# Residual add of the FFN by GpSimd, pieces of the Mamba chunks at other iterations, first chunk's load ahead of the weights, and strip rows one word longer

## The chip, the cores and the metric

The kernel runs on one core of a Trainium2 chip. A core has five engines with instruction streams of their own: TensorE (PE in the profile; its weight loads are PEld), VectorE (DVE), ScalarE (ACT), GpSimd (POOL) and SyncE (SP), which here only issues DMA transfers. They share an on-chip memory of 128 partitions (SBUF); TensorE writes to a second one (PSUM). The metric is the time of one execution on the device in microseconds (us); lower is better. Everything is computed in fp32.

## The reference, cut to what matters

The input x is 4 images of 64 channels and 128x128 pixels. Four layers follow each other:

```
layer 0: tokens of all images as ONE sequence of 65,536
         y = mamba(tokens, 16 states); p = proj(out_proj(y)); x = silu(layernorm(p)) + x
layer 1: q from the largest Sobel gradients; a windowed block transform by FFT, a block MLP
         with soft shrinkage, the transform back; + x
layer 2: r = relu(bn(conv3x3(relu(bn(conv3x3(x)))))); gate from means over cropped images;
         relu(r * gate + x)
layer 3: t = conv3x3(relu(conv3x3(x))) as tokens, 4 sequences of 16,384
         t = t + mamba(layernorm(t), 64 states)
         t = t + ffn(layernorm(t))       # 1x1 to 256, depthwise 3x3, GELU, 1x1 to 64
         x + t

mamba(u): xh, z = split(u @ in_w.T)                   # 128 channels each
          xc = silu(causal conv of 4 taps over xh)
          dt, B, C = split(xc @ x_proj.T)
          delta = softplus(dt @ dt_w.T + dt_b)
          h_t = h_{t-1} * exp(delta_t * A) + (delta_t * xc_t) B_t ;  y_t = h_t C_t
          (y + xc * D) * silu(z)
```

The recurrence in h runs over every channel and every state: 128 x 16 scans in layer 0, 128 x 64 in layer 3.

## The kernel before, in words

**Stages.** The layers run one after the other. In the profiled execution layer 0 lies at 0 to 3206 us, the gradients, window and transform of layer 1 at 3206 to 4280, the convolutions of layers 2 and 3 at 4283 to 5076, layer 3's Mamba at 5076 to 16,082, and its FFN at 16,082 to 17,159.

**The Mamba class.** Both Mamba layers use the class `_Mamba`. The tokens are cut into chunks of 1024, 64 chunks in each layer. An *iteration* is one scan instruction of VectorE (L640) over 1024 tokens on 128 partitions; these hold 4 states of 32 channels, and 4 iterations (j) make a *group* of 4 states of all 128 channels. A chunk has 16 iterations in layer 0 and 64 in layer 3. In each iteration ScalarE computes the decay `da` (an exponential, L595) up to six iterations ahead, TensorE brings the input term into a PSUM tile `bx`, VectorE scans it into a slot of `ring`, GpSimd multiplies the slot by the replicated C row (`cb`, L646), and TensorE later sums over the states into `y` (L470).

The input term has two kinds, written as a letter per group ("DADA" in layer 0, "DAAA" four times in layer 3). In a D group TensorE spreads B over the partitions (L533) and VectorE multiplies it by `du` (L539). In an A group the products with B are formed on transposed data: eight blocks of 128 tokens, each either one GpSimd instruction (L444, 512 elements) or four single ScalarE products (L440, 128 elements each), and then transposed by TensorE (L527). The number of blocks that GpSimd makes is `mine`: (2,) in layer 0, and (4, 2, 2) for the three A groups that follow a D group in layer 3.

Three PSUM tiles of 1024 columns (bx0 to bx2) are used in turn by the input terms and by the *pieces*: the matmuls that make the next chunk ready (convolution, z, delta, C, B, transposed du) or finish the last one (projection, LayerNorm). A piece is a generator: at a `yield` it hands over to the loop. `slots` gives, for each piece, the iteration after which it is issued, counted from the first iteration of its chunk: negative ones lie in the chunk before, those over 16 or 64 in the chunk after.

**What sets the order.** `run` writes the order out by hand, iteration by iteration: exponentials, products paced by a credit, the PSUM tiles to fill, the scan, GpSimd's product, y sums, pieces due, and replicated loads; `_Pin` fixes this order on each engine. All DMA transfers but those named below are issued by SP in program order.

**Front and start.** `front` computes xc (L321), sz (L330), pos (softplus, L339) and on GpSimd u = pos x xc (L347), and stores pos and u for the replicated loads. Its working tiles come from `tmp`. The constructor loads the weights by SP (L206 to L263, the 16 A_log transfers at L263 last), before anything of the first chunk. In layer 0 two chunks are then prepared ahead of the loop, in layer 3 one. Layer 3's `ahead` centres and normalises the tokens (on tile `nx`), and copies them by DMA into the convolution's input S; `behind` projects, adds the residual, normalises (tile `no`) and stores.

**Convolutions.** `layer2_convs3` works on strips of 16 rows. `strip` gives a tile of rows of 130 words (`RW` = 128 + 2). `_Conv.turned` forms four sums and differences V of rows, two on VectorE and two on GpSimd (L1233, L1235), which TensorE multiplies (L1247).

**FFN.** `layer3_ffn` has 32 strips of 16 rows. In each, hidden channels 128 to 255 are convolved by VectorE (`taps`, L1688 and eight L1686), the others by TensorE; `second` multiplies by fc2 and adds bias and residual (L1701) one strip later, and SP stores the result (L1704). `load` reads the normalised tokens two strips ahead (L1645). The residual tile `res` is loaded by SP from s3, and then x3 is added to it by four accumulating transfers issued by GpSimd (L1726). GpSimd then clears the borders of the next strip's hidden tile h (L1657, L1658, L1660), for which the next taps wait.

Of the kernel before, what the change touches and what calls it, by code (L numbers as in the profile page):

```python
# [10 lines left out]
F32 = mybir.dt.float32  # L11
AF = mybir.ActivationFunctionType
ALU = mybir.AluOpType
# [4 lines left out]
P = 128  # L18
B, C, HH, WW = 4, 64, 128, 128
HW = HH * WW  # L20
TC = 1024
# [149 lines left out]
class _Mamba:  # L171
# [18 lines left out]

    def __init__(self, ctx, tc, K, nst, w, kinds, bufs, slots={}):
        nc = self.nc = tc.nc
# [8 lines left out]

        self.slots = slots

        wx, xpd, dtw = (self.tmp(k)[:n, :DI] for k, n in (("wx", P), ("xpd", 4), ("dtw", 4)))
        for h in range(2):
# [15 lines left out]
        nc.sync.dma_start(self.wbc, w["xp_bcT"])  # L221
        self.small = nst <= DD
        self.wboth = cp.tile([P, NH, 64 if self.small else P], F32, name="wboth")
# [5 lines left out]
        self.spread = {}  # L229
        for g in (g for g, kind in enumerate(kinds) if kind == "D"):  # L230
# [74 lines left out]
    def tmp(self, name):  # L305
        return self.wp.tile([P, TC], F32, name=name, tag="tmp", bufs=self.bufs["tmp"])

# [170 lines left out]
    def run(self, chunks, ahead, behind, lead):  # L478
# [214 lines left out]
def layer0(ctx, tc, K, w, x, x1):  # L693
    nc = tc.nc
    slots = {"conv": -24, "z": -22, "v": -20, "C": -16, "B": -14, "duT": -12, "project": 32, "rstd": 34}
    m = _Mamba(ctx, tc, K, 16, w, "DADA", {"xc": 2, "sz": 3, "tmp": 4, "bc": 2, "soon": (), "da": 7, "made": 0, "mine": (2,)}, slots)
    cp, wp = m.cp, m.wp
    eps = cp.tile([P, 1], F32, name="eps")
    nc.vector.memset(eps, 1e-5)


    pw = cp.tile([64, 64], F32, name="pw")
    nc.sync.dma_start(pw, w["proj_w"])
    ow = cp.tile([64, DI], F32, name="ow")
    nc.sync.dma_start(ow, w["out_w"])
    pb = cp.tile([64, 1], F32, name="pb")
    nc.sync.dma_start(pb, w["proj_b"])
    pm = m.pm()
    nc.tensor.matmul(pm[:64, :64], pw, K.cent[:64, :64], start=True, stop=True)
    m1 = cp.tile([64, 64], F32, name="m1")  # L710
    nc.vector.tensor_copy(m1, pm[:64, :64])
    pm = m.pm()
    nc.tensor.matmul(pm[:, :64], ow, m1, start=True, stop=True)
    woT = cp.tile([P, 64], F32, name="woT")
    nc.vector.tensor_copy(woT, pm[:, :64])
    cent2 = cp.tile([64, P], F32, name="cent2")
    for h in range(2):
        nc.vector.tensor_copy(cent2[:, 64 * h : 64 * (h + 1)], K.cent[:64, :64])
    pm = m.pm()
    nc.tensor.matmul(pm[:, :1], cent2, pb, start=True, stop=True)  # L720
    ob = cp.tile([P, 1], F32, name="ob")
    nc.vector.tensor_copy(ob, pm[:, :1])
    lng = _dup(nc, cp, w["ln_g"], "lng")
    lnb = _dup(nc, cp, w["ln_b"], "lnb")

    finish = []
# [53 lines left out]

    chunks = [{"at": divmod(i * TC, HW), "reset": i == 0} for i in range(B * HW // TC)]
    m.run(chunks, ahead, behind, 24)
    flush()

# [491 lines left out]
def layer2_convs3(ctx, tc, K, w, w3, x2, x3, t3):  # L1276
# [202 lines left out]
def layer3_mamba(ctx, tc, K, w, t3, s3, n3):  # L1479

    nc = tc.nc
    slots = {"centre": -47, "norm": -45, "conv": -32, "conv2": -31, "z": -30, "v": -29, "C": -16, "B": -14, "duT": -12, "project": 80, "centre2": 82, "norm2": 84}
    m = _Mamba(ctx, tc, K, 64, w, "DAAADAAADAAADAAA", {"xc": 1, "sz": 2, "tmp": 4, "bc": 1, "soon": (), "da": 7, "made": 7, "mine": (4, 2, 2)}, slots)
    cp = m.cp
    eps = cp.tile([P, 1], F32, name="eps3")
    nc.vector.memset(eps, 1e-5)
    woT = cp.tile([P, 64], F32, name="woT")
# [10 lines left out]
    def load(c):  # L1498
        b, t0 = c["at"]
        X = c["X"] = m.t("X", 1, 512)  # L1500
        for h, src in enumerate(_halves(t3[b], t0)):
            nc.sync.dma_start(X[64 * h : 64 * (h + 1)], src)

    def ahead(c):
        if c is chunks[0]:
            load(c)
# [32 lines left out]
    def behind(c, yg):  # L1539
# [30 lines left out]

    chunks = [{"at": (b, t0), "reset": t0 == 0} for b in range(B) for t0 in range(0, HW, TC)]
    m.run(chunks, ahead, behind, 48)
# [3 lines left out]
def layer3_ffn(ctx, tc, K, w, n3, s3, x3, out):  # L1576
# [139 lines left out]
    for n, (b, r0) in enumerate(strips):  # L1716
# [6 lines left out]
        ximg = x3[b].rearrange("c (r w) -> c r w", w=WW)  # L1723
        for eng, img, add in ((nc.sync, simg, ALU.bypass), (nc.gpsimd, ximg, ALU.add)):
            for q in range(R // 4):
                eng.dma_start(res[half[q % 2], q // 2], img[:, r0 + 4 * q : r0 + 4 * q + 4, :], accum_op=add)  # L1726
        g0 = [wp.tile([P, 4, WW], F32, name=f"g0{q}", tag=f"g0{q}") for q in range(NR)]
# [129 lines left out]
```

## Time and profile before

| | |
|---|---|
| time, median of 3 runs | 17,136.39 us (17,125.25 to 17,164.81) |
| the profiled execution's own time | 17,161.19 us |
| its span | 17,159.4 us |
| busy: TensorE / VectorE / ScalarE / GpSimd | 80% / 89% / 80% / 81% |
| layer 0, a chunk | 48.65 us, VectorE idle 2.15 |
| layer 3 Mamba, a chunk | 170.66 us, VectorE idle 6.97 |
| FFN, a strip | 33.5 us |
| first scan of layer 0 / of layer 3 | 77.21 us / 5153.48 us |

The profile has one row for each group of instructions: line, engine, operation, output from inputs with their shapes, count, then busy time in all and mean ns of one, then the idle time before them and what ended most of it. A row of a timeline gives start and length in us, engine, line, operation, and in brackets how long the engine had waited and for what. A row of waits gives who waited for whom, the us in all, how often, and the longest. A row of windows gives the stretch, its length, and the busy time of each engine with the number of instructions.

### The profile page before, as it was taken

The page shows a single profiled execution, that of the slowest core. Times are in us where ns is not written, and L with a number is a line of the kernel's source. Part 1 is how long each engine was busy: PE and PEld are TensorE (multiplying, and loading weights), DVE is VectorE, ACT ScalarE, POOL GpSimd, SP SyncE. Part 2 cuts the span into 40 slices and gives each one's busy share as a digit, 9 for nine tenths or more (in the row PEclk, how much of TensorE's full clock was granted, in tenths as well). Part 3 has the DMA queues.
Part 4 walks back from the last instruction along what each step waited for, and adds up shares of the span by engine and source line. Part 5 has one row for each costly group of instructions (what it writes and reads, how often), then busy time and mean ns, then how long its engine had stood idle before and what let it go on. Part 6 is the DMA issues. An engine that isn't in the chain of part 4 may idle for free.

```text
span 17159.4 us, 249842 instructions
## 1 busy us (share of the span) xinstructions
PE 13728.5 (80%) x85562; PEld 7134.6 (42%) x85562; DVE 15207.3 (89%) x8587; ACT 13644.9 (80%) x27884; POOL 13844.1 (81%) x9954
## 2 busy tenths in 40 slices
PE   7888888899987777777777777777777777777766
PEld 3333333388434444444444444444444444444312
DVE  7999999732879999999999999999999999999766
ACT  7888888411539999999999999999999999999532
POOL 6888888501449999999999999999999999999511
PEclk8888888889999999999889999999999999999888
DMA  6666666311343333333333333333333333333233
GB/s 161 175 174 175 173 176 176 105 43 44 119 141 91 97 85 96 87 96 86 96 86 96 88 96 86 98 89 93 89 94 90 93 90 94 91 92 89 66 67 66
DMA packets 705600, 1779.59 MB, mean 104 GB/s; under 512 B 202481, under 2 KB 246465, under 8 KB 694849
## 3 DMA queue, kind: packets, MB, share of 16 engines
q1 hardware_dynamic: 694080, 1746.83, 37.4%
q0 software_dynamic: 10240, 16.79, 0.7%
q8 instruction: 672, 11.01, 0.3%
q14 instruction: 608, 4.97, 0.1%
HBM read 1439.91 MB, written 289.41 MB: 101 GB/s over the span
## 4 chain that ended last, share of the span: by engine, by line
PE 32%; DVE 26%; ACT 15%; issue 10%; DMA 7%; POOL 4%; SPq 4%; DVEq 0%; POOLq 0%; ACTq 0%
DVE ring L640 18%; ACT bxT L440 7%; PE y L470 7%; PE bx L527 6%; PE bx L300 5%; ACT da L595 5%; DVE bx L539 4%; DVE g L1686 3%; PE bx L533 3%; PE m L1247 3%; POOL ring L646 2%; DMA du<-d 2%; SPq L566 2%; DMA d<-pos 1%; DMA dl<-d 1%
## 5 line engine op out<-in xcount | busy, mean ns | idle before, releaser
L640 DVE TENSOR_TENSOR_SCAN ring<-da,state,bx 128x1024 f32<-128x1024 f32 x4848 | 11037.2, 2329 | 206.2 <-PE bx L527 110.3
L646 POOL TENSOR_TENSOR ring<-ring,cb 128x1024 f32<-128x1024 f32 x5120 | 10219.1, 2016 | 550.6 <-DVE ring L640 311.8
L440 ACT ACTIVATE bxT<-duT,BT 128x128 f32<-128x128 f32 x19456 | 6038.3, 389 | 23.7 <-PE bx L527 22.9
L595 ACT ACTIVATE da<-dl,A 128x1024 f32<-128x1024 f32 x5120 | 5732.2, 1139 | 362.6 <-DVE ring L640 347.0
L527 PE MATMUL bx<-cst,bxT 128*128 128x128 f32 x28672 | 4316.8, 298 | 1138.1 <-DVE ring L640 1047.7
L527 PEld LDWEIGHTS bx<-cst,bxT 128*128 128x128 f32 x28672 | 3771.9, 210 | 2616.7 <-DVE ring L640 1605.2
L470 PE MATMUL y<-ring,cst 128*32 128x512 f32 x20480 | 2971.1, 661 | 103.0 <-POOL ring L646 103.0
L444 POOL TENSOR_TENSOR bxT<-duT,BT 128x512 f32<-128x512 f32 x2304 | 2391.5, 1049 | 9.9 <-ACT BT L384 9.9
L533 PE MATMUL bx<-bc,spread 64*128 64x512 f32 (+1 forms) x6144 | 1810.0, 686 | 627.0 <-DVE ring L640 624.3
L539 DVE TENSOR_TENSOR bx<-du,bx 128x1024 f32<-128x1024 f32 x1536 | 1852.4, 1213 | 458.5 <-PE bx L533 315.6
L470 PEld LDWEIGHTS y<-ring,cst 128*32 128x32 f32 x20480 | 630.1, 117 | 1841.9 <-issue 1251.3
L533 PEld LDWEIGHTS bx<-bc,spread 64*128 64x128 f32 (+1 forms) x6144 | 523.3, 198 | 1730.3 <-DVE ring L640 1204.8
L300 PE MATMUL bx<-S,cw 128*128 128x512 f32 x1024 | 668.0, 813 | 376.4 <-DVE ring L640 363.2
L1726 POOL DMA_DIRECT2D res<-d_x x128 | 106.4, 1256 | 923.1 <-DMA res<-d_s 922.1
L1247 PE MATMUL m<-V,cw 64*64 64x512 f32 x6144 | 715.7, 604 | 87.9 <-POOL V L1233 49.0
L1137 POOL TENSOR_TENSOR xs<-xs,cl 128x1024 f32<-128x1024 f32 x32 | 75.9, 2372 | 795.8 <-DVE cl L1136 795.8
L1671 ACT ACTIVATE h<-ph,ff_fc_b 128x384 f32<-128x384 f32 (+1 forms) x384 | 200.4, 574 | 598.4 <-PE ph L1666 575.5
L640 DVE TENSOR_TENSOR_SCAN ring<-da,bx 128x1024 f32<-128x1024 f32 x272 | 602.6, 2267 | 20.4 <-PE bx L527 11.2
L1686 DVE SCALAR_TENSOR_TENSOR g<-h,dww,g 128x2048 f32<-128x2048 f32 x256 | 602.0, 2352 | 11.3
L300 PEld LDWEIGHTS bx<-S,cw 128*128 128x128 f32 x1024 | 257.3, 264 | 783.0 <-DVE ring L640 466.7
L1735 PE MATMUL pd<-h,diag 32*32 32x512 f32 x9216 | 376.9, 671 | 191.8 <-POOL h L1658 162.7
L1247 PEld LDWEIGHTS m<-V,cw 64*64 64x64 f32 x6144 | 331.4, 136 | 470.2 <-issue 342.9
(341 smaller groups left out, 10271.5 us busy)
## 6 DMA issues: line engine op xcount, KB each, us to landing
cb<-c SPq DMA_DIRECT2D x5120, 128.0 KB, 2.9
dl<-d SPq DMA_DIRECT2D x2048, 128.0 KB, 3.0
du<-d SPq DMA_DIRECT2D x2048, 128.0 KB, 3.8
d<-pos SPq DMA_DIRECT2D x128, 512.0 KB, 4.2
d<-u SPq DMA_DIRECT2D x128, 512.0 KB, 3.9
S<-nx SPq DMA_DIRECT2D x256, 128.0 KB, 2.4
S<-in_x SPq DMA_DIRECT2D x120, 256.5 KB, 4.1
res<-in_x SPq DMA_DIRECT2D x128, 128.0 KB, 2.9
```

The source lines that it names most:

```text
L300: self.nc.tensor.matmul(out[: l.shape[1], k : k + 512], l, r[:, k : k + 512], start=i == 0, stop=i == len(pairs) - 1)
L440: nc.scalar.activation(t[:, k, q].rearrange("p e j -> p (e j)"), c["duT"][:, k, :], AF.Copy, scale=c["BT"][:, k, n : n + 1])
L444: nc.gpsimd.tensor_mul(t[:, k].rearrange("p q e j -> p q (e j)"), c["duT"][:, k].unsqueeze(1).to_broadcast(shape), c["BT"][:, k, NQ * g : ...
L470: nc.tensor.matmul(c["y"][DD * j : DD * (j + 1), _COLS[h]], K.sel, hc[:, _COLS[h]], start=False, stop=u["g"] == self.ng - 1,)
L527: nc.tensor.transpose(bx[:, P * m : P * (m + 1)], v["bxT"][:, m, :, :, j].rearrange("p q e -> p (q e)"), self.K.eye)
L533: nc.tensor.matmul(bx[:, _COLS[h]], self.spread[v["g"]][r], self.rows(v["c"]["B"], h, 0), start=True, stop=True)
L539: nc.vector.tensor_mul(tiles[k], v["c"]["du"][j], tiles[k])
L595: nc.scalar.activation(das[nexp], v["c"]["dl"][k], AF.Exp, scale=self.A[:, k, v["g"] : v["g"] + 1])
L640: nc.vector.tensor_tensor_scan(hs, das.pop(i), tiles[i], 0.0 if u["c"].get("reset") else st, ALU.mult, ALU.add)
L646: nc.gpsimd.tensor_mul(hc, hs, u["cb"])
L1247: self.nc.tensor.matmul(p[k][i][half[h]], U[half[i], k, x, :], V[half[i], k, NP * h : NP * (h + 1), x : x + WW], start=x == 0, stop=x == 2,)
L1686: nc.vector.scalar_tensor_tensor(g1, tap, wk, g1, ALU.mult, ALU.add)
```

## The change: what it does

- FFN: x3 is loaded by SP into a tile `xin` of its own (four loads, after those of `res`), and one GpSimd addition over 128x1024 puts it into `res`, in place of the four accumulating transfers. `xin` begins two words off.
- Layer 0: pieces conv at -25 and its second half at -24 (one piece at -24 before), v at -21 (-20), and a lead of 26 iterations (24); GpSimd makes one of the eight blocks of an A group (two before).
- Layer 3: conv -33 and -32 (-32, -31), project 76 (80), centre2 80 (82); GpSimd makes 4, 1 and 2 blocks (4, 2, 2).
- Offsets: `cb` begins two words into its tile (one before); in layer 3 the tiles of `tmp` begin one word in, and the halves of `nx` and `no` lie one word apart (`split`).
- Starts: the constructor no longer loads weights; `weights` does. In layer 0 the first chunk's load comes before them and its `front` right behind them, ahead of the other constants. In layer 3 the LayerNorm weights, the first chunk's load and its `ahead` up to the convolution come first, then the weights.
- Convolutions: rows of a strip lie 131 words apart; 130 are used.

```diff
-    def __init__(self, ctx, tc, K, nst, w, kinds, bufs, slots={}):
+    def __init__(self, ctx, tc, K, nst, kinds, bufs, slots={}):
...
         self.slots = slots
-
+        self.small = nst <= DD
+
+    def weights(self, w):
+
+        nc, K, cp, nst = self.nc, self.K, self.cp, self.nst
         wx, xpd, dtw = (self.tmp(k)[:n, :DI] for k, n in (("wx", P), ("xpd", 4), ("dtw", 4)))
...
     def tmp(self, name):
-        return self.wp.tile([P, TC], F32, name=name, tag="tmp", bufs=self.bufs["tmp"])
+        k = self.bufs["shift"]
+        return self.wp.tile([P, TC + k], F32, name=name, tag="tmp", bufs=self.bufs["tmp"])[:, k:]
+
+    def split(self, name):
+
+        t = self.wp.tile([P, TC + 1], F32, name=name, tag="tmp", bufs=self.bufs["tmp"])
+        return t[:, :512], t[:, 513:]
...
     def _C(self, c, g):
-        t = self.t("cb", 3, TC + 1)[:, 1:]
+        t = self.t("cb", 3, TC + 2)[:, 2:]
...
         for c in chunks[:begun]:
-            for gen in (ahead, self.middle):
-                for _ in gen(c):
+            for gen in (c.pop("begun", None) or ahead(c), self.middle(c)):
+                for _ in gen:
                     pass
...
-    slots = {"conv": -24, "z": -22, "v": -20, "C": -16, "B": -14, "duT": -12, "project": 32, "rstd": 34}
-    m = _Mamba(ctx, tc, K, 16, w, "DADA", {"xc": 2, "sz": 3, "tmp": 4, "bc": 2, "soon": (), "da": 7, "made": 0, "mine": (2,)}, slots)
+    slots = {"conv": -25, "conv2": -24, "z": -22, "v": -21, "C": -16, "B": -14, "duT": -12, "project": 32, "rstd": 34}
+    m = _Mamba(ctx, tc, K, 16, "DADA", {"xc": 2, "sz": 3, "tmp": 4, "bc": 2, "soon": (), "da": 7, "made": 0, "mine": (1,), "shift": 0}, slots)
     cp, wp = m.cp, m.wp
...
+    chunks = [{"no": i, "at": divmod(i * TC, HW), "reset": i == 0} for i in range(B * HW // TC)]
+    load(chunks[0])
+    m.weights(w)
+    for _ in ahead(chunks[0]):
+        pass
+    chunks[0]["begun"] = iter([None])
+
     eps = cp.tile([P, 1], F32, name="eps")
...
     def ahead(c):
-        if c is chunks[0]:
-            load(c)
...
-    m.run(chunks, ahead, behind, 24)
+    m.run(chunks, ahead, behind, 26)
...
     def strip(tag, s, bufs):
 
-        t = wp.tile([P, SR + 2, RW], F32, name=tag, tag=tag, bufs=bufs)
+        t = wp.tile([P, SR + 2, RW + 1], F32, name=tag, tag=tag, bufs=bufs)[:, :, :RW]
...
 def layer3_mamba(ctx, tc, K, w, t3, s3, n3):
 
     nc = tc.nc
-    slots = {"centre": -47, "norm": -45, "conv": -32, "conv2": -31, "z": -30, "v": -29, "C": -16, "B": -14, "duT": -12, "project": 80, "centre2": 82, "norm2": 84}
-    m = _Mamba(ctx, tc, K, 64, w, "DAAADAAADAAADAAA", {"xc": 1, "sz": 2, "tmp": 4, "bc": 1, "soon": (), "da": 7, "made": 7, "mine": (4, 2, 2)}, slots)
+    slots = {"centre": -47, "norm": -45, "conv": -33, "conv2": -32, "z": -30, "v": -29, "C": -16, "B": -14, "duT": -12, "project": 76, "centre2": 80, "norm2": 84}
+    m = _Mamba(ctx, tc, K, 64, "DAAADAAADAAADAAA", {"xc": 1, "sz": 2, "tmp": 4, "bc": 1, "soon": (), "da": 7, "made": 7, "mine": (4, 1, 2), "shift": 1}, slots)
...
-    woT = cp.tile([P, 64], F32, name="woT")
-    nc.sync.dma_start(woT, w["out_wT"])
-
     g1, b1 = (_dup(nc, cp, w[k], f"{k}_") for k in ("ln1_w", "ln1_b"))
-    m.shift(b1)
...
-        no = m.tmp("nx")
-        xs, sq = no[:, :512], no[:, 512:]
+        xs, sq = m.split("nx")
...
-        no = m.tmp("no")
-        xs, o = no[:, :512], no[:, 512:]
+        xs, o = m.split("no")
...
+    load(chunks[0])
+    begun = chunks[0]["begun"] = ahead(chunks[0])
+    while next(begun) != m.slot(chunks[0], "conv"):
+        pass
+    m.weights(w)
+    m.shift(b1)
+    woT = cp.tile([P, 64], F32, name="woT")
+    nc.sync.dma_start(woT, w["out_wT"])
     m.run(chunks, ahead, behind, 48)
...
         ximg = x3[b].rearrange("c (r w) -> c r w", w=WW)
-        for eng, img, add in ((nc.sync, simg, ALU.bypass), (nc.gpsimd, ximg, ALU.add)):
+        xin = wp.tile([P, 2 * 4 * WW + 2], F32, name="xin", tag="xin")[:, 2:].rearrange("p (k r w) -> p k r w", k=2, w=WW)
+        for t, img in ((res, simg), (xin, ximg)):
             for q in range(R // 4):
-                eng.dma_start(res[half[q % 2], q // 2], img[:, r0 + 4 * q : r0 + 4 * q + 4, :], accum_op=add)
+                nc.sync.dma_start(t[half[q % 2], q // 2], img[:, r0 + 4 * q : r0 + 4 * q + 4, :])
+        nc.gpsimd.tensor_add(res, res, xin)
```

More of the change, by code (lines that the diff above doesn't have):

```diff
@@ L221, in __init__ @@
         nc.sync.dma_start(self.wbc, w["xp_bcT"])
-        self.small = nst <= DD
         self.wboth = cp.tile([P, NH, 64 if self.small else P], F32, name="wboth")
@@ L229, in __init__ @@
         self.spread = {}
-        for g in (g for g, kind in enumerate(kinds) if kind == "D"):
+        for g in (g for g, kind in enumerate(self.kinds) if kind == "D"):
             s = self.spread[g] = cp.tile([P, P], F32, name=f"spread{g}")
@@ L694, in layer0 @@
     nc = tc.nc
-    slots = {"conv": -24, "z": -22, "v": -20, "C": -16, "B": -14, "duT": -12, "project": 32, "rstd": 34}
-    m = _Mamba(ctx, tc, K, 16, w, "DADA", {"xc": 2, "sz": 3, "tmp": 4, "bc": 2, "soon": (), "da": 7, "made": 0, "mine": (2,)}, slots)
+    slots = {"conv": -25, "conv2": -24, "z": -22, "v": -21, "C": -16, "B": -14, "duT": -12, "project": 32, "rstd": 34}
+    m = _Mamba(ctx, tc, K, 16, "DADA", {"xc": 2, "sz": 3, "tmp": 4, "bc": 2, "soon": (), "da": 7, "made": 0, "mine": (1,), "shift": 0}, slots)
     cp, wp = m.cp, m.wp
[L698 to L713, printed above, removed]
-    woT = cp.tile([P, 64], F32, name="woT")
[L715 to L724, printed above, removed]
     finish = []
@@ L779, in behind @@
         finish.append(last)
-    chunks = [{"at": divmod(i * TC, HW), "reset": i == 0} for i in range(B * HW // TC)]
-    m.run(chunks, ahead, behind, 24)
+    chunks = [{"no": i, "at": divmod(i * TC, HW), "reset": i == 0} for i in range(B * HW // TC)]
[4 more added lines that the diff above has]
+    chunks[0]["begun"] = iter([None])
+    eps = cp.tile([P, 1], F32, name="eps")
+    nc.vector.memset(eps, 1e-5)
+    pw = cp.tile([64, 64], F32, name="pw")
+    nc.sync.dma_start(pw, w["proj_w"])
+    ow = cp.tile([64, DI], F32, name="ow")
+    nc.sync.dma_start(ow, w["out_w"])
+    pb = cp.tile([64, 1], F32, name="pb")
+    nc.sync.dma_start(pb, w["proj_b"])
+    pm = m.pm()
+    nc.tensor.matmul(pm[:64, :64], pw, K.cent[:64, :64], start=True, stop=True)
+    m1 = cp.tile([64, 64], F32, name="m1")
+    nc.vector.tensor_copy(m1, pm[:64, :64])
+    pm = m.pm()
+    nc.tensor.matmul(pm[:, :64], ow, m1, start=True, stop=True)
+    woT = cp.tile([P, 64], F32, name="woT")
+    nc.vector.tensor_copy(woT, pm[:, :64])
+    cent2 = cp.tile([64, P], F32, name="cent2")
+    for h in range(2):
+        nc.vector.tensor_copy(cent2[:, 64 * h : 64 * (h + 1)], K.cent[:64, :64])
+    pm = m.pm()
+    nc.tensor.matmul(pm[:, :1], cent2, pb, start=True, stop=True)
+    ob = cp.tile([P, 1], F32, name="ob")
+    nc.vector.tensor_copy(ob, pm[:, :1])
+    lng = _dup(nc, cp, w["ln_g"], "lng")
+    lnb = _dup(nc, cp, w["ln_b"], "lnb")
+    m.run(chunks, ahead, behind, 26)
     flush()
@@ L1486, in layer3_mamba @@
     nc.vector.memset(eps, 1e-5)
-    woT = cp.tile([P, 64], F32, name="woT")
-    nc.sync.dma_start(woT, w["out_wT"])
     g1, b1 = (_dup(nc, cp, w[k], f"{k}_") for k in ("ln1_w", "ln1_b"))
-    m.shift(b1)
     pad = cp.tile([P, 1], F32, name="pad")
@@ L1504, in ahead @@
     def ahead(c):
-        if c is chunks[0]:
-            load(c)
         t0 = c["at"][1]
         S = m.t("S", 1, TC + 3)
-        no = m.tmp("nx")
-        xs, sq = no[:, :512], no[:, 512:]
+        xs, sq = m.split("nx")
         yield m.slot(c, "centre")
@@ L1569, in behind @@
             nc.sync.dma_start(_halves(n3[b], t0)[h], o[64 * h : 64 * (h + 1)])
-    chunks = [{"at": (b, t0), "reset": t0 == 0} for b in range(B) for t0 in range(0, HW, TC)]
+    at = [(b, t0) for b in range(B) for t0 in range(0, HW, TC)]
+    chunks = [{"no": i, "at": a, "reset": not a[1]} for i, a in enumerate(at)]
+    load(chunks[0])
[4 more added lines that the diff above has]
+    m.shift(b1)
+    woT = cp.tile([P, 64], F32, name="woT")
+    nc.sync.dma_start(woT, w["out_wT"])
     m.run(chunks, ahead, behind, 48)
```

## The prediction

> **What bounds the kernel now.** I read the page's engine totals and its groups first, then windows inside the two Mamba stages and the FFN, then the waits in those windows, and last the timeline of the start-ups and of one FFN strip. The sum below is made against the profiled execution (span 17,159.4 us, its own time 17,161.2); the median of the runs shown, 17,136.4, lies 25 us under it.
>
> ```profile
> PE 13728.5 (80%) x85562; PEld 7134.6 (42%) x85562; DVE 15207.3 (89%) x8587; ACT 13644.9 (80%) x27884; POOL 13844.1 (81%) x9954
> ...
> L640 DVE TENSOR_TENSOR_SCAN ring<-da,state,bx 128x1024 f32<-128x1024 f32 x4848 | 11037.2, 2329 | 206.2 <-PE bx L527 110.3
> L646 POOL TENSOR_TENSOR ring<-ring,cb 128x1024 f32<-128x1024 f32 x5120 | 10219.1, 2016 | 550.6 <-DVE ring L640 311.8
> L440 ACT ACTIVATE bxT<-duT,BT 128x128 f32<-128x128 f32 x19456 | 6038.3, 389 | 23.7 <-PE bx L527 22.9
> ...
> L444 POOL TENSOR_TENSOR bxT<-duT,BT 128x512 f32<-128x512 f32 x2304 | 2391.5, 1049 | 9.9 <-ACT BT L384 9.9
> ```
>
> The first row averages unlike stages. The windows (us, then busy of PE, PEld, DVE, ACT and POOL) separate them:
>
> ```profile
> 200.00:3000.00 2800.00, 2403.44 (x12300) 1078.81 (x12302) 2676.79 (x1440) 2451.10 (x4540) 2354.89 (x1551) 0.89 0.67 175
> 6000.00:15000.00 9000.00, 7083.40 (x40695) 3775.79 (x40697) 8630.46 (x4272) 8284.93 (x17875) 8732.40 (x6225) 0.91 0.34 91
> 16150.00:17100.00 950.00, 653.59 (x9514) 189.60 (x9512) 611.14 (x315) 306.53 (x493) 114.80 (x243) 0.83 0.31 65
> ```
>
> In layer 0 (first row) VectorE is busy 96% and nothing else is near it. In layer 3's Mamba, which is 11,006 us of the kernel, VectorE is at 96% and GpSimd at 97%. A chunk of 1024 tokens there takes 170.66 us, in which VectorE has 163.7 us of work, GpSimd 165.6, ScalarE 157.2. In layer 0 a chunk takes 48.65 us: VectorE 46.5, ScalarE 42.8, GpSimd 41. So only VectorE's gaps can be won, 6.97 us a chunk in layer 3 and 2.15 in layer 0, 64 chunks each. Who ends those gaps, in the waits of the layer 3 window (52.7 chunks; us in all, times, longest):
>
> ```profile
> DVE bx L539 <- PE bx L533: 198.4, 186, 3.6
> ...
> DVE ring L640 <- PE bx L527: 93.3, 149, 1.6
> ACT bc L371 <- PE bx L533: 93.2, 52, 2.8
> ...
> PE y L470 <- POOL ring L646: 80.1, 56, 2.3
> ...
> DVE ring L640 <- PE y L470: 50.8, 66, 1.6
> ```
>
> All VectorE waits name TensorE: a piece of the next or last chunk (conv, z, v, project) or a y matmul stood before the bx tile. 1.5 us a chunk of it goes back to GpSimd, for whose product L470 waits. By place in the chunk, the layer 3 gap is 1.46 us before scan 19 (project, centre), 1.74 before 32 (y behind a late GpSimd), 2.05 before 34 to 37 (conv, z, v), 0.77 before 44 (GpSimd late after its 2.37 us product L347), about 0.95 elsewhere.
>
> In the FFN (third row) no engine is full: a strip of 16 rows takes 33.5 us, of which VectorE's nine taps are 20.5, and then it waits 11.6. This is the timeline of that wait (start, length):
>
> ```profile
> 16606.44 1.40 DVE L1701 SCALAR_TENSOR_TENSOR o<-po,fc2b__121306,res 128x512 f32<-128x512 f32 x2
> ...
> 16607.21 2.40 SPq L1704 DMA_DIRECT2D out<-o  x4
> 16609.71 1.18 SPq L1645 DMA_DIRECT2D N<-d_n  x2
> 16611.07 2.38 SPq L1726 DMA_DIRECT2D res<-d_s  x4
> ...
> 16615.71 3.31 POOL L1726 DMA_DIRECT2D res<-d_x  x4 [28.05 <-DMA res<-d_s]
> ...
> 16619.45 0.12 POOL L1658 MEMSET h<- 128x18 f32 x1
> ...
> 16619.50 1.28 DVE L1688 TENSOR_SCALAR g<-h,dww 128x2048 f32<-128x2048 f32 x1 [11.66 <-POOL h L1660]
> ```
>
> The stores wait for L1701, the loads stand behind the stores on SP's queue, GpSimd's accumulating transfers wait for the loads, the memsets of h are behind them in GpSimd's order, and the next taps wait for the memsets. The loop closes through this chain.
>
> **The change part by part.**
>
> *Layer 3, steady.* Of 48 A blocks (L444) per 16 groups, one is dropped in each of four groups: GpSimd loses 4 x 1.05 = 4.2 us a chunk; ScalarE gains 16 products L440, whose pitch when back to back is 6038.3/19456 = 0.31, so 5.0 us. The displaced words change operand offsets modulo 32 bytes. Rows show what that does to GpSimd: operands at one offset take 2371 ns (L347, 1024 elements), 4 bytes apart 2016 (L646), 8 apart 2088 for 1040 elements, shortest about 2015 (L1233). So L347 gains 0.35 us a chunk, the two 512-element LayerNorm products 0.25 each, and L646 (4 to 8 bytes apart) 0 to 0.03 each, 64 a chunk; I take 0.02, 1.3 us. GpSimd: 165.6 - 4.2 - 0.35 - 0.5 - 1.3 = 159.3. ScalarE: 157.2 + 5.0 = 162.2. VectorE, 163.7, is then the fullest. The project piece goes to four iterations earlier, apart from the centre pieces, and conv one earlier. Expected gaps: 1.46 becomes 0.76, 1.74 becomes 0.3, 2.05 becomes 1.7, 0.77 becomes 0.3, the rest stays: 3.0 us less a chunk, x 63 = -190. Bounds: all that GpSimd and the pieces cause, -300; nothing, 0; beyond that a loss, in the rivals. ScalarE must fit: today it waits 13.5 us a chunk, 5.0 for VectorE (it is ahead) and 8.45 for TensorE's pieces; 162.2 leaves 5.5 of a 167.7 us chunk. It meets most of those pieces early because it runs ahead; later arrival shortens the wait. That is the assumption on which this part stands.
>
> *Layer 0, steady.* GpSimd does one block less in each of two groups, ScalarE 8 x 0.31 = 2.5 us more (45.3), hidden while below 46.5 plus gaps. The conv's matmuls, now split in two, are issued before the tile that today waits 1.05 us for them; z and v come together, which in layer 3 costs about 0.8. Of 2.15, 1.05 + 0.53 + 0.15 go and 0.85 comes: -0.9 x 62 = -56 (0 to -95).
>
> *Start-ups.* Layer 0: the first chunk's load is issued at 20.9 (SP's row S<-in_x in the timeline), behind all weight loads; it goes first, and conv of chunk two (45.15) can run at about 28, -17. Every weight load then moves back by the S load's first issues. Layer 3: X's load is at 5098.1 behind 8.4 us of A loads; moved ahead, conv goes from 5114.65 to about 5098, less 1.5 us for ScalarE's table change between xc and sz, since A's exponential now stands there: -15. S's copies are queued among the A loads, which A's exponential awaits; still covered by the 30 us to the first scan. Bounds for the two together: -10 to -40.
>
> *Convolutions.* Rows of 131 words bring GpSimd's V operands (L1235, 2911 ns) from 16 to 8 bytes apart, as L1233 has (2088): 0.7 us in 64 V. TensorE is over 91% busy there and waits for V 49 us in three places; I take -8 (0 to -49).
>
> *FFN.* SP issues four more loads (as L1726 by SP, 2.38), GpSimd waits for their landing (2.25 from the last issue, as at 16,613.45 to 16,615.7 for res), adds 128x1024 (L646's 2.0) and does the memsets (0.35): 7.0 us in place of 2.25 + 3.55 (accumulation's start to L1688). +1.2 x 31 = +37. Bounds +15 (loads land together) to +75.
>
> Two rules bear on this add. The Trainium skill (GPSIMD Engine Reference, Performance versus the Vector engine) has elementwise work on VectorE, GpSimd being about half as fast: 4497 ns for 2048 elements, so an estimated 2.25 for 1024. L646 shows 2.02, and L539 1.21 for VectorE; placed there it would save 0.8 x 31 = 25 us. It is a cost within the +37. And its page SBUF — State Buffer (Who interferes with whom) says that a VectorE instruction with two SBUF inputs and a GpSimd one that reads SBUF block each other. A tap L1686 is such, 2.35 us; if the add met one every strip the part would be +37 + 73 = +110. L1235 beside VectorE's own V sums (2911 against 2088) fits the rule. I take none of it: the add stands in the 11.6 us in which VectorE waits for the very memsets behind it.
>
> Sum: -190 - 56 - 17 - 15 - 8 + 37 = -249; 17,161 - 249 = 16,912, and against the median 17,136 - 249 = 16,887: **16,890**.
>
> **The rivals.** *ScalarE becomes the bound (slower).* If its 8.45 us of waits for pieces stay, a layer 3 chunk is 162.2 + 8.45 = 170.65, no gain, and layer 0's 45.3 + 5.5 = 50.8, +2.1 x 63 = +135; with FFN and starts +135 + 37 - 32 - 8 = +132: 17,270. It decides where waits exceed 8.4 us a chunk in layer 3 and 3.3 in layer 0. For it: those waits are in today's trace. Against: VectorE's own progress sets most. *GpSimd's relief is taken up elsewhere:* TensorE's pieces, by name 5.5 of VectorE's 6.97 us, stay (L539 3.75, L640 on L527 1.76), and layer 3 gains 0 to 1.3 us: 16,990 to 17,090, say 17,040. *All of GpSimd's share goes* and L646 loses its full 30 ns: 16,700. *Eight bytes apart is as bad as zero:* 0.35 x 64 = 22 us more on GpSimd a chunk, about +900; L1233's 2015 speaks against it. *The moves do nothing:* a new start order hidden by the same later chain, 30 us worse, within the range.
>
> **How the numbers follow.** Forecast .52, small relief .23, all gaps .05; ScalarE .15, a bad offset .02, no change from small gains and the FFN's upper bound .03. A run of this kernel tells about 0.2%, 34 us, from no change (17,102 to 17,171). A few of the small-relief cases fall there: faster .76, same .07, slower .17. Own range of the forecast 16,760 to 17,000; for 8 in 10 with the small relief: 16,740 to 17,120.
>
> **What would show it.** Layer 3 chunk near 167.7 with GpSimd at about 159 and ScalarE 162; DVE waits on y L470 nearly gone; layer 0 chunk near 47.75 with no xc wait before scan 11; FFN strip near 34.7 with GpSimd's add of about 2 us ahead of the memsets; the two first scans 17 and 15 us earlier in their stages. It is wrong if ScalarE's waits for TensorE keep their 8 us beside more work, if L646's mean leaves 1.98 to 2.02, or if the add meets the taps.

## The result and the profile after

The changed kernel takes 17,177.99 us in the median (17,170.96 to 17,187.85, 20 runs), the kernel before 17,141.88 (17,125.04 to 17,166.82, 20 runs) beside it: a ratio of 1.002, interval 1.0013 to 1.0026. It is slower by 0.2%, where 16,890 and a gain of 1.5% were forecast, and it lies above the range given (16,740 to 17,120). The profiled execution has a span of 17,178.2 us.

Where the time went, by landmarks of the two traces (first and last scan of each Mamba, first and last TensorE product of the convolutions, first tap's start and last tap's end in the FFN; us):

| stretch | before | after | difference | forecast |
|---|---|---|---|---|
| start to layer 0's first scan | 77.2 | 65.2 | -12.0 | -17 |
| layer 0's scans | 3109.8 | 3104.4 | -5.5 | -56 |
| from there to the convolutions | 1105.9 | 1104.9 | -1.0 | 0 |
| convolutions | 781.6 | 779.0 | -2.5 | -8 |
| from there to layer 3's first scan | 79.0 | 65.7 | -13.3 | -15 |
| layer 3's scans | 10,914.0 | 10,912.8 | -1.2 | -190 |
| last scan to the first tap | 42.4 | 40.4 | -2.0 | 0 |
| FFN, first to last tap | 1030.1 | 1087.0 | +56.9 | +37 |
| rest | 19.5 | 18.9 | -0.6 | 0 |
| sum (span) | 17,159.4 | 17,178.2 | +18.8 | -249 |

The medians stand 36 us apart and the spans 19, because the profiled execution of the kernel before lies high among its runs. The scans of the two Mamba layers gave 7 of the 246 us expected of them, and the FFN lost half as much again as expected. These are the engine totals and three groups of the page after (L649 is the scan, L655 GpSimd's product, L1742 the new addition):

```profile
PE 13632.2 (79%) x85562; PEld 7089.7 (41%) x85562; DVE 15189.9 (88%) x8587; ACT 14071.2 (82%) x29421; POOL 13389.9 (78%) x9474
...
L649 DVE TENSOR_TENSOR_SCAN ring<-da,state,bx 128x1024 f32<-128x1024 f32 x4848 | 11039.3, 2330 | 387.0 <-PE bx L536 204.0
L655 POOL TENSOR_TENSOR ring<-ring,cb 128x1024 f32<-128x1024 f32 x5120 | 10233.2, 2014 | 1023.9 <-DVE ring L649 680.3
...
L1742 POOL TENSOR_TENSOR res<-res,xin 128x1024 f32<-128x1024 f32 x32 | 66.7, 2084 | 1027.9 <-DMA xin<-d_x 998.6
```

GpSimd has 454 us less to do and ScalarE 426 more; GpSimd's product now waits 1023.9 us in place of 550.6, mostly for the scan. GpSimd was relieved and VectorE went no faster. The windows of the same stages say it once more (us, then busy of PE, PEld, DVE, ACT, POOL):

```profile
200.00:3000.00 2800.00, 2410.75 (x12356) 1045.93 (x12360) 2682.91 (x1442) 2596.41 (x5022) 2260.49 (x1444) 0.89 0.67 175
6000.00:15000.00 9000.00, 6992.79 (x40712) 3769.54 (x40716) 8620.20 (x4273) 8512.09 (x18723) 8510.36 (x6014) 0.92 0.34 92
16150.00:17100.00 950.00, 612.38 (x8856) 177.37 (x8856) 578.63 (x297) 285.58 (x459) 72.96 (x154) 0.82 0.26 62
```

In layer 3 VectorE is busy for 8620 us of 9000, against 8630 before; GpSimd comes to 161.4 us a chunk and ScalarE to 161.4 (159.3 and 162.2 forecast). A chunk takes 170.69 us (170.66 before), and its idle time is 7.19 us (6.97). It has only changed places (us a chunk, by the scan before which VectorE stood idle, waits over 0.05 us summed from the trace over 61 chunks):

| place in the chunk | before | forecast | after |
|---|---|---|---|
| before 19 to 21 (project, centre) | 1.46 | 0.76 | 1.54 |
| before 32 | 1.74 | 0.3 | 0.89 |
| 34 to 38 (conv, z, v) | 2.05 | 1.7 | 1.51 |
| before 44 | 0.77 | 0.3 | 2.24 |

And these are VectorE's waits of the layer 3 window after:

```profile
DVE bx L548 <- PE bx L542: 135.5, 132, 1.9
DVE ring L649 <- PE y L479: 124.8, 70, 3.1
DVE ring L649 <- PE bx L536: 93.2, 79, 2.0
```

The wait for the D groups' tile fell from 198.4 to 135.5, and the scan's wait for the y sums rose from 50.8 to 124.8. The gain at the D groups and at 34 to 38 is real and is lost again at one scan of the chunk, the 44th. In layer 0 a chunk takes 48.54 (48.65).

The FFN's loop, by the timeline after (start, length):

```profile
16599.58 0.59 SPq L1659 DMA_DIRECT2D N<-d_n  x1
16600.21 2.51 SPq L1741 DMA_DIRECT2D res<-d_s  x4
16602.82 2.46 SPq L1741 DMA_DIRECT2D xin<-d_x  x4
16608.66 1.99 POOL L1742 TENSOR_TENSOR res<-res,xin 128x1024 f32<-128x1024 f32 x1 [31.74 <-DMA xin<-d_x]
...
16610.83 0.21 POOL L1674 MEMSET h<- 128x130 f32 x1
...
16611.07 1.28 DVE L1702 TENSOR_SCALAR g<-h,dww 128x2048 f32<-128x2048 f32 x1 [13.96 <-POOL h L1674]
```

The order is the one foreseen: the four loads of xin behind those of res, the add for their landing, the memsets behind the add, the taps behind the memsets. VectorE's wait is 13.96 us here. From the first tap of one strip to that of the next it is 35.30 us, 33.53 before (mean without the two strips at either end; all strip times below are counted so).

### The profile page after: what moved, and what is told of

The parts are those of the page before. It is cut to its first block, busy times and chain, and to the rows that moved or that the text cites. A ratio compares the mean times of both kernels' runs of the same rounds, so it can differ in the third digit from the quotient of the medians.

```text
span 17178.2 us, 250822 instructions
## 1 busy us (share of the span) xinstructions
PE 13632.2 (79%) x85562; PEld 7089.7 (41%) x85562; DVE 15189.9 (88%) x8587; ACT 14071.2 (82%) x29421; POOL 13389.9 (78%) x9474
## 5 line engine op out<-in xcount | busy, mean ns | idle before, releaser
L649 DVE TENSOR_TENSOR_SCAN ring<-da,state,bx 128x1024 f32<-128x1024 f32 x4848 | 11039.3, 2330 | 387.0 <-PE bx L536 204.0
L655 POOL TENSOR_TENSOR ring<-ring,cb 128x1024 f32<-128x1024 f32 x5120 | 10233.2, 2014 | 1023.9 <-DVE ring L649 680.3
L449 ACT ACTIVATE bxT<-duT,BT 128x128 f32<-128x128 f32 x20992 | 6502.7, 390 | 24.3 <-PE bx L536 23.5
L542 PE MATMUL bx<-bc,spread 64*128 64x512 f32 (+1 forms) x6144 | 1868.3, 698 | 804.6 <-DVE ring L649 804.3
L453 POOL TENSOR_TENSOR bxT<-duT,BT 128x512 f32<-128x512 f32 x1920 | 1990.7, 1051 | 10.7 <-ACT BT L393 10.7
L1742 POOL TENSOR_TENSOR res<-res,xin 128x1024 f32<-128x1024 f32 x32 | 66.7, 2084 | 1027.9 <-DMA xin<-d_x 998.6
L649 DVE TENSOR_TENSOR_SCAN ring<-da,bx 128x1024 f32<-128x1024 f32 x272 | 602.3, 2268 | 29.8 <-PE y L479 12.8
L1700 DVE SCALAR_TENSOR_TENSOR g<-h,dww,g 128x2048 f32<-128x2048 f32 x256 | 605.3, 2364 | 11.3
L303 PE MATMUL bx<-S,cw 128*128 128x512 f32 x1024 | 480.2, 611 | 2.6 <-DMA S<-nx 1.4
L377 PE MATMUL bx<-xc,wboth 128*64 128x512 f32 (+1 forms) x512 | 334.6, 1008 | 143.5 <-DVE ring L649 142.2
```

The source lines that it names most:

```text
L303: self.nc.tensor.matmul(out[: l.shape[1], k : k + 512], l, r[:, k : k + 512], start=i == 0, stop=i == len(pairs) - 1)
L449: nc.scalar.activation(t[:, k, q].rearrange("p e j -> p (e j)"), c["duT"][:, k, :], AF.Copy, scale=c["BT"][:, k, n : n + 1])
L453: nc.gpsimd.tensor_mul(t[:, k].rearrange("p q e j -> p q (e j)"), c["duT"][:, k].unsqueeze(1).to_broadcast(shape), c["BT"][:, k, NQ * g : ...
L542: nc.tensor.matmul(bx[:, _COLS[h]], self.spread[v["g"]][r], self.rows(v["c"]["B"], h, 0), start=True, stop=True)
L649: nc.vector.tensor_tensor_scan(hs, das.pop(i), tiles[i], 0.0 if u["c"].get("reset") else st, ALU.mult, ALU.add)
L655: nc.gpsimd.tensor_mul(hc, hs, u["cb"])
```

## The experiments

The theory after the result had three parts. (1) In layer 3, the 44th scan writes the ring slot that the y sums of iterations 36 to 39 read, so it waits for them; they stand on TensorE behind a tile that now waits for ScalarE, and ScalarE is late because of the moves (which of them, the runs were to tell). (2) In layer 0, z and v, now in one place, cost what the split convolution gained. (3) In the FFN, the strip's loop closes through the residual. Each ratio below is to the kernel before, run beside it, whose median then lay between 17,148 and 17,162. Rivals were ScalarE's extra products (the mechanism of the prediction's slower rival, at one place), GpSimd, and contention between the add and the taps.

This is the stretch before the 44th scan in one chunk of the kernel after (the wait is 2.68 us here, 2.24 in the mean of all chunks):

```profile
7270.32 3.98 POOL L655 TENSOR_TENSOR ring<-ring,cb 128x1024 f32<-128x1024 f32 x2
...
7273.14 1.13 ACT L604 ACTIVATE da<-dl,A 128x1024 f32<-128x1024 f32 x1
7274.18 3.31 ACT L449 ACTIVATE bxT<-duT,BT 128x128 f32<-128x128 f32 x11
...
7275.13 0.72 PE L536 MATMUL bx<-cst,bxT 128*128 128x128 f32 x4 [1.10 <-DVE ring L649]
7276.37 0.39 PE L536 MATMUL bx<-cst,bxT 128*128 128x128 f32 x1 [0.52 <-ACT bxT L449]
...
7277.54 0.92 PE L536 MATMUL bx<-cst,bxT 128*128 128x128 f32 x3 [0.79 <-ACT bxT L449]
...
7278.39 3.64 PE L479 MATMUL y<-ring,cst 128*32 128x512 f32 x16
...
7282.15 4.59 DVE L649 TENSOR_TENSOR_SCAN ring<-da,state,bx 128x1024 f32<-128x1024 f32 x2 [2.68 <-PE y L479]
```

TensorE transposes the last tile block by block as ScalarE's eleven products arrive, up to 7277.49. Only then do the 16 y products start, and the scan waits for their end. GpSimd's product of iteration 39, the second in the first row, had been done since 7274.30.

The kernel before has the same queue, and the prediction laid its wait to GpSimd. One of its chunks:

```profile
6635.85 3.98 POOL L646 TENSOR_TENSOR ring<-ring,cb 128x1024 f32<-128x1024 f32 x2
...
6637.50 3.31 ACT L440 ACTIVATE bxT<-duT,BT 128x128 f32<-128x128 f32 x11
...
6641.70 3.64 PE L470 MATMUL y<-ring,cst 128*32 128x512 f32 x16
...
6645.46 4.59 DVE L640 TENSOR_TENSOR_SCAN ring<-da,state,bx 128x1024 f32<-128x1024 f32 x2 [1.57 <-PE y L470]
```

GpSimd is done at 6639.83, and the y products start 1.87 us later; in all 47 chunks with a wait there of over 0.1 us it is 1.82 to 1.94. ScalarE's eleven products end 5.95 us after the 40th scan's start in this chunk, 7.06 in the one after.

**One y sum earlier.** `run` has a parameter `soon` for groups whose y sums go one iteration earlier; it was empty.

```diff
-{"xc": 1, "sz": 2, "tmp": 4, "bc": 1, "soon": (), "da": 7, "made": 7, "mine": (4, 1, 2), "shift": 1}
+{"xc": 1, "sz": 2, "tmp": 4, "bc": 1, "soon": (40,), "da": 7, "made": 7, "mine": (4, 1, 2), "shift": 1}
```

> The changed kernel with one y sum per chunk (group of iterations 36 to 39) issued one iteration earlier, ahead of the tile for 44 on TensorE instead of behind it; nothing else. Theory: VectorE's 44th scan waits for these sums, because it writes the ring slot that they read, and they stand behind a tile that waits for ScalarE's products; moved ahead, 1.5 to 2 us of the 2.24 go: 95 to 125 us, 17,050 to 17,085. Rival, the sums wait for GpSimd's product and not for the tile: they wait as long in the new place, the tile behind them comes later, and the time stays or rises by up to 60 us.

Measured: 17,032.35 us (17,030.15 to 17,036.36), ratio to the kernel before 0.9929, interval 0.9914 to 0.9944. The chunk falls from 170.69 to 168.28, the scans of layer 3 by 150 us. The same stretch of that run:

```profile
7244.80 13.51 DVE L649 TENSOR_TENSOR_SCAN ring<-da,state,bx 128x1024 f32<-128x1024 f32 x6
...
7248.33 2.75 PE L479 MATMUL y<-ring,cst 128*32 128x512 f32 x16
7248.54 3.32 ACT L449 ACTIVATE bxT<-duT,BT 128x128 f32<-128x128 f32 x11
...
7251.02 2.50 PE L536 MATMUL bx<-cst,bxT 128*128 128x128 f32 x16
```

The y products go first, in the time in which TensorE would wait for ScalarE, and six scans follow each other without a gap. The wait before 44 is gone altogether, a little more than the theory had set. That the sums waited for their place on TensorE, and not for GpSimd, is shown. (The time lies 18 us under the expected range.)

**The blocks back.**

```diff
-"mine": (4, 1, 2)
+"mine": (4, 2, 2)
```

> The changed kernel with layer 3's blocks as before (4, 2, 2), its piece positions kept. Theory: the 16 more products make ScalarE late in iterations 39 to 43, the tile for 44 waits for them and the y sums behind it; with them gone VectorE's wait before 44 falls from 2.24 to about 0.8 us a chunk. The wait before 32, where GpSimd is late, rises from 0.9 to about 1.7, so the chunk goes from 170.69 to 170 or 170.2: minus 30 to 45 us, about 17,140. Rival, the moved pieces cause the wait before 44: it stays near 2.2 and the time rises by the wait before 32, 50 us, to 17,230.

Measured: 17,163.18 us (17,158.20 to 17,170.02), ratio 1.0006 (0.9996 to 1.0015). The wait before 44 stays at 2.11 us, so ScalarE's 16 extra products a chunk are not what makes it late there: my theory's expectation failed and the rival's first half held. Its second half did not: with GpSimd burdened again the wait before 32 rises only from 0.89 to 1.00, those at 19 to 21 and at 34 to 38 fall by 0.2 and 0.4, and the chunk takes 170.44, 0.25 us less. In this order of pieces GpSimd's relief bought nothing in layer 3; it cost a little. No run has the blocks back with the 44th scan's wait gone.

**The convolution pieces back.**

```diff
-"conv": -33, "conv2": -32,
+"conv": -32, "conv2": -31,
```

> The changed kernel with layer 3's convolution pieces back at -32 and -31; project and centre stay moved, and so do the blocks. Theory: exponentials are held back from xc to pos, so conv one iteration earlier leaves one more of them (1.14 us) for the rush after pos, the products for the tile before 44 come 1.1 us later, and the y sums behind that tile with them. Put back, VectorE's wait before 44 falls from 2.24 to 0.8 us and the one before 34 to 38 rises from 1.5 to about 2.0: the chunk goes from 170.69 to 169.3 to 169.9, 50 to 90 us less, 17,090 to 17,130. Rival, moving project and centre did it: the wait before 44 stays at 2.2, and the time is 17,180 to 17,215.

Measured: 17,204.72 us (17,194.47 to 17,215.39), ratio 1.0026 (1.0017 to 1.0035). The chunk is 170.92. VectorE's waits in the layer 3 window of this run:

```profile
DVE bx L548 <- PE bx L542: 178.0, 160, 1.7
DVE ring L649 <- PE bx L536: 160.6, 122, 4.8
DVE ring L649 <- PE y L479: 22.6, 28, 1.1
```

The wait for y falls from 124.8 to 22.6, that is before 44 from 2.24 to 0.63 us a chunk: the convolution's move did cause it. But the waits at 34 to 38 rise from 1.51 to 3.49, where I had 2.0. So the move is worth 2.0 us a chunk at its own place and costs 1.6 at the 44th scan. The rival (project and centre) is out for the wait, though its total came nearer; the total was decided by the term that I had too small. Why it is 3.49 stays open: conv stands where it stood in the kernel before, and there it was 2.05. Most of the excess lies before scan 36, where 18 of the 61 chunks wait 2.6 to 4.8 us and the others about 1.4; so the other moves cost something there with conv at its old place, and no run parts them.

How conv comes to delay ScalarE is read from the traces. `run` holds exponentials back from xc until pos. With conv one iteration earlier the hold begins one exponential sooner: three of them follow pos in the kernel before, four in the kernel after, and the thirteen and eleven products behind them come that much later. In the two chunks shown above, before and then after:

```profile
6629.52 3.24 ACT L595 ACTIVATE da<-dl,A 128x1024 f32<-128x1024 f32 x3
```

```profile
7265.16 4.27 ACT L604 ACTIVATE da<-dl,A 128x1024 f32<-128x1024 f32 x4
```

The 40th exponential is done 15.84 us ahead of its scan before, 4.11 after, and 16.75 with conv back (means of 61 chunks). No run lifts the hold itself.

**Layer 0's v piece back.**

```diff
-"v": -21,
+"v": -20,
```

> The changed kernel with layer 0's v piece back at -20, z kept at -22, so that one tile stands between them on TensorE again. Theory: z and v in one place are what VectorE waits for before scan 13 (1.42 us a chunk), v waiting for a PSUM tile that ScalarE's sz gives back; apart, this falls to 0.3 and the split conv's gain stays: a chunk from 48.54 to 47.5 or 47.8, 45 to 65 us less, 17,113 to 17,133. Rival, VectorE waits for v wherever it is put, and the wait moves to scan 15: chunk 48.4 to 48.7, no change.

Measured: 17,135.75 us (17,127.87 to 17,139.68), ratio 0.9982 (0.9972 to 0.9992). A chunk of layer 0 takes 47.79 us, its scans 3052.4 in all, 52 less than after; the time is 3 us above the expected range. VectorE's waits in the layer 0 window, in the kernel after and then in this run:

```profile
DVE ring L649 <- PE bx L536: 95.2, 71, 2.8
DVE bx L548 <- PE bx L542: 6.6, 37, 0.2
```

```profile
DVE ring L649 <- PE bx L536: 33.0, 59, 0.7
DVE bx L548 <- PE bx L542: 20.7, 117, 0.2
```

The longest wait falls from 2.8 to 0.7 us. Without a tile between them z and v hold up scan 13 by 1.42 us a chunk; with one between them that wait is gone. Part of it comes back at the scans 3, 6 and 8, whose waits grow from 0.44 to 1.02 us together, so a chunk gains 0.75; why they grow was not followed.

**Layer 0's blocks back.**

```diff
-"da": 7, "made": 0, "mine": (1,), "shift": 0
+"da": 7, "made": 0, "mine": (2,), "shift": 0
```

> The changed kernel with layer 0's blocks as before (2 by GpSimd, 24 products by ScalarE in place of 28). Theory: ScalarE has room there and the moved block costs nothing, so nothing changes: chunk 48.4 to 48.7, 17,168 to 17,188. Rival, the eight more products a chunk (2.5 us) are what ate the gain of the moved pieces: the chunk falls by 0.5 to 1 us, 30 to 60 us less, 17,115 to 17,150.

Measured: 17,186.69 us (17,179.42 to 17,196.06), ratio 1.0014 (1.0005 to 1.0023); chunk 48.57. No change: ScalarE has room for its 2.5 us more, and gains nothing by it.

**The FFN's residual back.** The four lines of `xin` in the diff are replaced by the two loops of before.

> The changed kernel with the FFN's residual as before (four accumulating transfers by GpSimd). Theory: the strip's loop closes through the residual, and the change put 1.8 us into it (SP's four more loads 2.68, 0.69 more to the landing, 1.42 less from there to the taps). The FFN falls by 56 us, a strip from 35.2 to 33.5, and nothing else moves: about 17,122, some 20 under the kernel before. Rival, the FFN is slower because the taps meet the add: the same total here, but then the taps' mean of 2364 ns falls and the time from the stores to the taps does not.

Measured: 17,125.02 us (17,120.15 to 17,133.21), ratio 0.9985 (0.9976 to 0.9995). First to last tap takes 1030.1 us (1087.0 after, 1030.1 before). The whole loss of the change lies in this part; all the rest of it gains 0.15%. The rival is out but for one strip: in the kernel after, the taps of all strips but the first take 2352 ns as they do here, and in the first, where two adds meet them, two taps take 3.97 us, which is 3.2 us once.

**The add behind the memsets.**

```diff
-        nc.gpsimd.tensor_add(res, res, xin)
...
         for _ in ahead:
             pass
+        nc.gpsimd.tensor_add(res, res, xin)
         nc.scalar.activation(g1, g1, AF.Gelu, bias=dwb1)
```

> The changed kernel with GpSimd's add issued behind the memsets of the next strip's h instead of ahead of them; the loads stay where they are. Theory, the loop closes through the residual: now the memsets no longer wait for it, VectorE's 11 to 14 us idle per strip go for the most part, and the strip comes down to what TensorE needs, 23.0 us, plus the waits around it: 25 to 28 us, 220 to 300 us less, 16,880 to 16,960. Rival, the add meets the taps and each blocks the other: taps longer by up to 2.0 us a strip, so 27 to 30 us a strip, 17,010 to 17,100. Rival, the loads on SP's queue and not the add hold the strip: no more than 2 us a strip, 17,115.

Measured: 16,833.44 us (16,829.61 to 16,837.20), ratio 0.9813 (0.9798 to 0.9827). A strip takes 23.23 us in place of 35.30, below the 25 to 28 expected. The loop did close through the residual. The groups of this run from 16,150 to 16,700 us show the next price:

```profile
L1700 DVE SCALAR_TENSOR_TENSOR g<-h,dww,g 128x2048 f32<-128x2048 f32 x189 | 483.1, 2556 | 8.3
...
L1764 POOL TENSOR_TENSOR res<-res,xin 128x1024 f32<-128x1024 f32 x24 | 77.7, 3236 | 480.4 <-DMA xin<-d_x 421.6 <-ACT h L1685 39.8 <-DVE g L1700 19.0
```

Beside the taps the add takes 3.24 us instead of 2.00, and a tap 2556 ns in the mean instead of 2352, 1.6 us a strip. (2.08 and 2364, which are used in the next expectation, are means of the kernel after with the strip in which the two met.) A tap that no add meets takes 2352 here too, so the rival was right in kind, with 1.6 us where it set up to 2.0. From 16,150 to 16,750 us VectorE is busy for 591 of 600.

**The old residual behind the memsets.**

```diff
         for _ in ahead:
             pass
+        for q in range(R // 4):
+            nc.gpsimd.dma_start(res[half[q % 2], q // 2], ximg[:, r0 + 4 * q : r0 + 4 * q + 4, :], accum_op=ALU.add)
         nc.scalar.activation(g1, g1, AF.Gelu, bias=dwb1)
```

(res is loaded by SP as before; there is no xin and no addition.)

> The changed kernel with the residual of before (four accumulating transfers by GpSimd, no addition), these issued behind the memsets of the next strip's h. Set beside the add put there (16,833; strip 23.85, taps 2556 ns in place of 2364, the add 3.24 us in place of 2.08). Theory: the place in GpSimd's order decides, and the add's own price, once it lies beside the taps, is the 1.5 us a strip by which it slows them; without it taps are at 2364 again and a strip is 22.2 to 22.5: 16,785 to 16,795. Rival, the transfers' issue also blocks VectorE or lands too late: taps stay slow or L1715 waits, and the time is 16,830 or more.

Measured: 16,786.04 us (16,785.29 to 16,787.71), ratio 0.9781 (0.9767 to 0.9796); a strip takes 21.68 us. (The expectation counted its strips from the diagonals' making at L1639, ahead of the first tap; so counted, this run has 22.30.) Its groups in the same window:

```profile
L1700 DVE SCALAR_TENSOR_TENSOR g<-h,dww,g 128x2048 f32<-128x2048 f32 x203 | 477.4, 2352 | 8.9
...
L1763 POOL DMA_DIRECT2D res<-d_x x100 | 82.7, 1253 | 447.7 <-DMA res<-d_s 360.0 <-DVE g L1700 87.8
```

The taps are at full pace again. That the taps are slowed by the add itself, and not by GpSimd's issuing transfers beside them, is shown; the add in place of the transfers is a loss of 1.55 us a strip in this place as it was of 1.8 in the other.

**Together.** The three gains in one kernel: the transfers behind the memsets, `soon` (40,), layer 0's v at -20.

> The changed kernel with three edits together: accumulating transfers behind the memsets (no addition), layer 3's y sum of iterations 36 to 39 one iteration earlier, layer 0's v at -20. If they lie in stages of their own, as the theory has it, their gains add up: 392 + 146 + 42 off 17,178, so 16,590 to 16,605. If a later bound takes part of one, the sum falls short by over 20 us.

Measured: 16,583.13 us (16,579.79 to 16,585.33), ratio to the kernel before 0.9671, interval 0.9657 to 0.9684. The gains add up: 595 us off 17,178, where their sum was 580. That is 7 us under the expected range.

**Layer 3's v one later,** on top of that:

```diff
-"z": -30, "v": -29,
+"z": -30, "v": -28,
```

> The kernel of the run before it, with layer 3's v piece one iteration later (-28 in place of -29), so that a tile stands between z and v as in layer 0. Theory: z and v together are the 1.47 us wait before scan 37 or 38, and apart it falls by about 1 us a chunk: 60 us less, 16,530 to 16,545. Rival: exponentials are held until pos, so a later v leaves one more of them for the rush behind it, and VectorE waits for ScalarE's products in 40 to 44 instead: no gain, or a loss of up to 100 us.

Measured: 16,655.41 us (16,654.33 to 16,659.18), ratio 0.9714 (0.9701 to 0.9727): 72 us more. VectorE's waits in layer 3 in the kernel with three edits, and then with this one:

```profile
DVE bx L548 <- PE bx L542: 137.2, 110, 3.3
DVE ring L649 <- PE bx L536: 86.9, 73, 2.0
```

```profile
DVE bx L548 <- PE bx L542: 142.1, 127, 1.8
DVE ring L649 <- PE bx L536: 128.3, 150, 2.2
```

The 1.47 us at z and v go, as expected of them, and 1.91 come back at the 44th scan, as the rival said: the 40th exponential is now done 1.03 us ahead of its scan. What is right in layer 0 is wrong in layer 3, where a hold on exponentials hangs on the same piece.

## Why the prediction was wrong, by its own steps

- *Layer 3, the gaps (-190, measured -1).* The step that failed is the list "1.46 becomes 0.76, 1.74 becomes 0.3, 2.05 becomes 1.7, 0.77 becomes 0.3". The last term was given to GpSimd ("late after its product L347"), whose product was done 1.8 us and more before the sums began. It was the place of the y sums on TensorE, behind a tile that waits for ScalarE, and the moved convolution made it worse: 2.24 where 0.3 was put. I had priced conv's move only at its own place. The question left unasked was what ScalarE does between xc and pos, and what comes late behind it. Of the other terms, 32 gave 0.85 of the 1.44 put on it and 34 to 38 gave 0.54 where 0.35 was put; the first did not fall (1.54), so parting project from the centre pieces shows no gain, though no run takes that move back alone.
- *GpSimd's relief.* 6.3 us a chunk were worked out and 4.2 came, the blocks' share; the offsets gave 0.4 at the LayerNorm products, nothing at u, and L655 took 0.2 more in the window. It was worth nothing here: 97% busy before, but not what the scans waited for last. The run with the blocks back shows it.
- *ScalarE must fit.* In sum it did: its waits for TensorE's pieces fell from 8.4 to 6.4 us a chunk, those for VectorE from 5.0 to 2.6. The slower rival (ScalarE full, 17,270) did not come about. But the room over a chunk says nothing of the five iterations in which ScalarE has a queue. There it was late by one exponential.
- *Layer 0 (-56, measured -5.5).* The mechanism was right and two terms were mis-sized: z and v together cost 1.42 us in place of 0.85, and the wait before scan 6 (0.15), which was to go, grew to 0.21. The waits before scans 11 and 0 went, as forecast. That the chunk is 47.79 with v apart, where 47.75 was forecast with z and v together, is luck: the 1.42 us are gone and other waits have grown. (ScalarE's 42.8 us a chunk should have been 42.6; nothing hung on it.)
- *Starts (-32, measured -25) and convolutions (-8, measured -2.5).* Right in kind. L1235's sums (now L1248) take 2316 to 2536 ns, where 2088 was expected.
- *FFN (+37, measured +57).* The path was right, two terms too small: SP's loads add 2.68 us, not 2.38, and the wait from the last issue to the add is 2.95, not 2.25. The add and memsets take 2.13, a little less than the 2.35 put down. The add did not meet the taps after the first strip, as argued, since VectorE waited for the memsets behind it. Seen from here the larger matter was in the same timeline: VectorE's 11.6 us idle were one misplaced instruction, whichever way the residual is added.
- *Operand offsets.* L655 takes 2014 ns (2016 before), nothing; 1.3 us a chunk had been counted.

The rivals: "GpSimd's relief is taken up elsewhere" was the nearest, but it kept a gain of 0 to 1.3 us in layer 3, layer 0's gain in full, and so ended at 17,040. The slower outcome came from small gains lost at two scans plus the FFN's loss, a sum to which I had given 3 in 100.

## What to carry to other kernels

When a piece is moved in a hand-written order, follow every rule that hangs on it (here, a hold on exponentials until another piece is read) and ask what each engine does in the iterations behind it; a share of busy time over a chunk shows no queue of 4 us. A wait that names TensorE is asked twice: what did that instruction itself wait for, and what stood ahead of it. And where an engine idles for a memset, see what is ahead of the memset in its queue: moving the residual behind it was worth 345 us, and exchanging it for another form of itself had cost 57.

## What the runs showed that was not expected

- GpSimd's add and VectorE's taps, which both read two operands of SBUF, hold each other up. With the add beside them, in 31 of 32 strips one of the eight taps takes 3.90 to 3.97 us and the other seven 2.35, so 1.6 us more in all; the add, 2.00 us alone, takes 2.0 to 4.1. The Trainium skill (SBUF — State Buffer, Who interferes with whom) says that such a pair contends for a shared port that only one holds at a time, and this agrees in kind; the price is less than the 2.35 us (one tap) that the prediction worked out from it.
- Four accumulating transfers issued by GpSimd during the taps did not slow them (2352 ns).
- GpSimd's product depends on which operand lies further. With the offsets that the program gives (the tiles taken to begin at multiples of 32 bytes; the traces hold no addresses), in0 4 bytes behind in1 modulo 32 gives 1094 to 1107 ns for 512 elements (1285 to 1295 at equal offsets); in0 4 bytes ahead gives 2374 for 1024 in layer 3, hardly better than equal offsets (2383). So u = pos x xc gained nothing from its shift, and nx and no gained 0.19 us each.
